# Four attention and aggregation layers on one core: loads, held instructions and idle-time products at three layer passages

## The chip, the cores and the metric

The kernel runs on one core of a Trainium2 chip. The metric is the device time of one execution in microseconds (us). Before the change the median of three runs is 3238.4 us (3236.99 to 3240.71). One more execution, the one that the hardware profiler recorded, took 3230.94 us; all durations quoted from the profile belong to it.

The engines are named as in the profile: PE (TensorE, the matrix engine), DVE (VectorE), ACT (ScalarE), POOL (GpSimd) and SP (SyncE). Each works through its own list of instructions in a fixed order. POOL and SP issue most of the DMA transfers here.

## The reference

A graph of 3327 nodes with 512 features each passes four layers. After each layer the result is added to the layer's input and every row is normalised (mean and variance over the 512 features, no scale or shift). With `x` [3327, 512] and `adj` [3327, 3327] of zeros and ones:

```python
# layers 0, 2 (8 heads of 64) and 3 (4 heads of 128): graph attention
Wh = h @ W                                   # per head
e = leaky_relu(f1[:, :, None] + f2[:, None, :], 0.2)   # f1 = Wh.a1, f2 = Wh.a2
att = softmax(where(adj > 0, e, -9e15), axis=-1)
out = att @ Wh                               # layers 2 and 3: elu(out)
# layer 1: mean over the first 64 neighbours of each row, two linear maps
keep = Ab & (cumsum(Ab, axis=1) <= 64)
xj = leaky_relu((keep @ X) / max(cnt, 1) @ W_nb.T + b_nb)
out = leaky_relu(X @ W_line.T + b_line) + where(cnt > 0, xj, 0)
# after every layer
x = layernorm(x + out)
```

## The kernel before

**Tiles.** Rows are padded to 26 tiles of 128 (`NT` = 26, `HALF` = 13, `IW` = 1664 = 13 tiles). A tile of node features is 128 x 512 in float32.

**An attention layer** (L0, L2 and L3) has a projection stage and an attention stage. In the projection stage each tile is transposed on PE through the identity matrix (`project1`, L267, buffer `pt`), copied to SBUF by ACT (L268, `xT`) and multiplied by the weights `wsb` (`project2`, L277, 16 products into the banks `pw0` and `pw1`). ACT then takes the last columns as exponents and copies (`dc` L278, `rc` and `qc` L281), and DVE scales the projected rows (`vt`, L283). In the attention stage of L0 and L2 (`unit8`, L791 and on) eight units run one after another; each has 26 steps j over the source tiles. Per step DVE makes the weighted mask `t` (L833), ACT the second factor `y` (L834), PE multiplies `t` into four accumulators `po` (L855, 16 products) and `y` into the denominators `pd` (L811). Units 1 to 6 take one head for all 26 target tiles; the first and the last unit, 0 and 7, take two heads (k = 0 and 1) for one half of the targets, so that a step has two DVE and two ACT instructions of half width. At the end of a unit the accumulators are copied (`ob`, L870), transposed by PE (L875), copied (`hb`, L882) and stored to the DRAM tensor `hd` by SP (L886). After the last unit the denominators are transposed on DVE (L948, L951), reduced (L955), written to DRAM (`dd`, L957) and read back (`pes`, L967).

**The norm between layers** is in `finish_steps` (L164 and on): load a tile `h` from `hd` and the residual `xr`, multiply `h` by the reciprocal denominators (`divide`, L182), for layer 2 an exponential on ACT (`e`, L189), add the residual (L197 and L198 for layer 2, L200 for layer 0), and then `norm_rows` for two tiles at once: statistics on DVE (L152, L153), square root on ACT (L154), reciprocal (L155) and the product with the mean (L158) on DVE, and the normalisation of each tile on ACT (L161, one instruction a tile). The buffers of the two last factors are called `rs`.

**The passages.** A passage is the stretch in which one stage's end and the next stage's start overlap.
- L0 to layer 1 (950 to 990 us): the function `sage`, first part. Per tile PE transposes (L1185), and multiplies by the neighbour weights `wn` (`pz`, L1193) and the line weights `wl` (`pi`, L1196), four products each; ACT copies `pz` (L1197), DVE makes the rest `zs` (L1198) and the line result `xi` (L1200 to L1202). Weights, residual rows and the carries `cy` (L1123) are loaded through POOL's queue, tiles 4 and on of `h` and the neighbour mask `mb` (L1140) through SP's.
- Layer 1 to L2 (1600 to 1635 us): `sage`, second part. Row blocks are summed on PE (`acc`, L1295); as each tile is finished (`output`), two jobs transpose and project it for L2. After the last tile come `mean` (`pm`, L299; in the profile under the bank's name `pw`) and unit 0 of L2.
- L2 to L3 (2388 to 2445 us): the function `third`. PE alternates between the transpose of a tile (L267) and the projection of an earlier one (L277). Tiles are loaded up to three pairs ahead (`load_group`), tiles 2 and 3 through POOL's queue, the others through SP's; the residuals and `wsb` come through POOL's. In the step of tile 14, `L3.prepare` clamps and exponentiates the row factors `rc` of the first 13 tiles (L315, L318) and transposes them through the identity in groups (`quad`, L324 to L327).

**What sets the order.** The program records instructions; a list scheduler then sets each engine's order from its own estimates, and may move an instruction ahead of others that were recorded earlier. `tc.keep_in_program_order(ins)` holds an instruction: held instructions of one engine keep the order in which they were recorded among themselves. Before the change the divisions (L182) of a call with `pinned` set are held when `t0 > 2`: those are tiles 4 to 7 of layer 0's norm, which `sage` calls with `t0 < 6`. In `third` only the first exponential of tile 2 is held.

Of the kernel before, what the change touches and what calls it, by code (L numbers as in the profile page):

```python
# [7 lines left out]
F32 = mybir.dt.float32  # L8
# [5 lines left out]
ALU = mybir.AluOpType  # L14
# [4 lines left out]
P = 128  # L19
# [13 lines left out]
def kernel(  # L33
# [111 lines left out]

    def norm_rows(pool, ys, t0):
        n = len(ys)
        st = pool.tile([P, 4, 6], F32, name="st")
        mv = pool.tile([P, 4, 2], F32, name="mv")
        rs = pool.tile([P, 4, 2], F32, name="rs")  # L150
        for s, y in enumerate(ys):
            nc.vector.bn_stats(out=st[:, s, :], in_=y)  # L152
            nc.vector.bn_aggr(out=mv[:, s, :], in_=st[:, s, :])  # L153
        nc.scalar.activation(rs[:, :n, 0], mv[:, :n, 1], AF.Sqrt, bias=eps)  # L154
        nc.vector.reciprocal(rs[:, :n, 0], rs[:, :n, 0])  # L155
        if t0 + n == NT:
            nc.vector.tensor_tensor(rs[:, n - 1, 0:1], rs[:, n - 1, 0:1], valid, op=ALU.mult)
        nc.vector.scalar_tensor_tensor(rs[:, :n, 1], mv[:, :n, 0], -1.0, rs[:, :n, 0],  # L158
                                       op0=ALU.mult, op1=ALU.mult)
        for s, y in enumerate(ys):  # L160
            nc.scalar.activation(y, y, AF.Identity, bias=rs[:, s, 1:2], scale=rs[:, s, 0:1])  # L161
# [3 lines left out]
    def finish_steps(pool, xin, layer, t0, n, hbufs=6, eng=nc.sync, xbufs=None, xpool=None, ebufs=None, pinned=False,  # L165
# [14 lines left out]
        def divide(s):  # L180
# [3 lines left out]
                                          op=ALU.mult)  # L184
            if pinned and t0 > 2:
                tc.keep_in_program_order(ins)
# [18 lines left out]
        else:  # L205
            for s in range(n):
                steps += [lambda s=s: divide(s), lambda s=s: add(s)]
        steps.append(lambda: norm_rows(pool, ys, t0))
        return ys, steps
# [581 lines left out]
    def unit8(self, pools, n, ring, background, aside, ending=None):  # L791
# [47 lines left out]
        for j in range(NT):  # L839
# [4 lines left out]
            if j not in made:  # L844
                js = (j, j + 1) if not u.wide and j in (0, NT - 2) else (j,)
                for j_ in js:
                    made[j_] = tp.tile([P, 2, IW], F32, name="t"), yp.tile([P, 2, IW], F8, name="y")
                for k in range(1 if u.wide else 2):
                    for j_ in js:
                        weights(j_, *made[j_], k)  # L850
# [254 lines left out]
    def sage(first, first_pool, xin, prev, nxt, wsrc, dst, ring):  # L1105
# [5 lines left out]
        with tc.tile_pool(name="sg_z", bufs=1, reuse_waits="tile") as zp, \  # L1111
# [14 lines left out]

            load_carry()
            load_carry()
            zs_ = [zp.tile([P, HALF, 2, F], F32R, name=f"zs{i}") for i in range(2)]
# [40 lines left out]

            for t in range(0, NT, 2):
                load_block(0, t)
            with tc.tile_pool(name="sa_w", bufs=1, reuse_waits="tile") as wp, \
# [5 lines left out]
                blb = wp.tile([P, F], F32, name="blb")  # L1179
                nc.gpsimd.dma_start(out=blb, in_=bl.to_broadcast([P, F]))  # L1180

                def step1(xt):
# [28 lines left out]
                for t0 in range(0, NT, 2):  # L1211
                    ys = ahead
                    if t0 in (6, 10):
                        prev.late.pop(0)(fp)
                    if t0 == 8:
                        cf = fp.tile([NT, P], F32, name="cf", bufs=1)
# [33 lines left out]
            with tc.tile_pool(name="sb_w", bufs=1, reuse_waits="tile") as wp, \  # L1250
# [38 lines left out]
                for b in range(len(blocks)):  # L1289
                    t0, i0 = blocks[b]  # L1290
                    for s in range(G):
# [18 lines left out]

                        def job1(y=y, t=t0 + s, held=held):
                            held["xT"] = nxt.project1(sp, ps, y, t, t < NT - 2)

# [17 lines left out]
    def third(first):  # L1331
        with tc.tile_pool(name="col3", bufs=1) as cp:
# [5 lines left out]
            with tc.tile_pool(name="p_w", bufs=1, reuse_waits="tile") as wp, \  # L1338
# [21 lines left out]
                nc.vector.tensor_copy(wsb[:, :, :, FW:], wa[3].rearrange("p c (e h) -> p c e h", e=2))  # L1360
                load_group(4)
                for t0 in range(0, NT, 2):
                    ys = ahead
# [3 lines left out]
                    for s, y in enumerate(ys):  # L1367
# [10 lines left out]
                        if t == HALF + 1:  # L1378
                            L3.prepare(pp, 0)
                            L3.first_rows = L3.rows(rp, 0, 0)  # L1380
                            L3.cut(pp, 0, "pc", 1, False, True)
# [339 lines left out]
```

## Time and profile before

| | |
|---|---|
| median of three runs | 3238.4 us (3236.99 to 3240.71) |
| the profiled execution | 3230.94 us |
| its span in the profile | 3229.1 us |
| mean granted PE clock | 0.987 of full speed |
| busy share of PE / DVE / ACT / POOL | 97 / 81 / 71 / 8 % |
| waits of PE in 950 to 990 us | 5.5 for `wn`, 1.2 for `h` of L161, 0.5 for `hb`, 0.3 for `xT` |
| waits of PE in 1600 to 1740 us | 3.6 for `rc`, 3.0 for `t`, 1.2 for `pd`, 0.7 for `xT`, 0.7 for `vt` |
| waits of PE in 2395 to 2432 us | 11.2 for `h` of L161, 1.3 for `xr`, 0.2 for `hb` |

The profiled execution lies 7.5 us below the median of the timed runs; times are therefore compared like with like, and a difference worked out in the profile is added to the median. In a timeline row the columns are the start, the duration from the first start to the last end, the engine, the line and operation, the tile written and the tiles read with their shapes, the number of instructions in the row (xN), and in square brackets the idle time of the engine just before it with what ended it. In a list of waits the three numbers after the colon are the sum of the idle time, the number of times and the longest one. An engine's clock in a stretch is given as a share of full speed.

### The profile page before, as it was taken

To read this page: it belongs to the slowest core of one execution; us is meant where nothing else is said; L and a number is where in the kernel's file an instruction comes from. 1 tells how busy PE (TensorE), PEld (TensorE's weight loads), DVE (VectorE), ACT (ScalarE), POOL (GpSimd) and SP (SyncE) were. 2 spreads that over 40 slices of the span, in tenths; PEclk is the share of its full clock that TensorE was granted. 3 is DMA by queue.
4 is the path that set the end of the run, shared out by engine and by line. 5 is a ranking of instruction groups with operands and counts; after the bars stand their busy time and mean duration, and the time that the engine had idled before them with its cause. 6 is when DMAs were issued, how large, how long until landed. Compare 5 with 4: busy or idle time off the path is not lost. (4 is left out here: it accounts for less than half of the span.)

```text
span 3229.1 us, 44980 instructions
## 1 busy us (share of the span) xinstructions
PE 3137.4 (97%) x17910; PEld 1602.3 (50%) x17910; DVE 2626.5 (81%) x2316; ACT 2295.1 (71%) x1855; POOL 266.6 (8%) x414
## 2 busy tenths in 40 slices
PE   8899999999999999999999999999989999999997
PEld 7643343333334467777744333333347655555444
DVE  5799999999987655555499999999999666677887
ACT  1388888899883234444398988899988655568896
POOL 3110000000000111111220000000011000010110
PEclk9999999999999999999999999999999999999998
DMA  9742113111024345555441111011137211122212
GB/s 360 272 149 80 41 51 137 59 45 42 25 87 138 104 127 133 134 142 152 120 135 42 41 35 39 20 42 42 32 107 242 85 43 43 43 59 89 85 47 69
DMA packets 358321, 301.80 MB, mean 93 GB/s; under 512 B 232756, under 2 KB 291966, under 8 KB 356575
## 3 DMA queue, kind: packets, MB, share of 16 engines
q1 hardware_dynamic: 325727, 187.73, 19.9%
q0 software_dynamic: 26864, 103.50, 10.0%
q10 hardware_dynamic: 5520, 7.69, 0.7%
q8 instruction: 142, 2.33, 0.3%
q14 instruction: 68, 0.56, 0.1%
HBM read 221.97 MB, written 76.84 MB: 93 GB/s over the span
## 5 line engine op out<-in xcount | busy, mean ns | idle before, releaser
L834 ACT ACTIVATE y<-t,bi,sc 128x3328 fp8e4<-128x3328 f32 (+1 forms) x520 | 1336.9, 2604 | 100.0 <-PE pd L811 47.8
L855 PE MATMUL po<-t,vj 128*64 128x448 f32 (+1 forms) x6656 | 1272.9, 522 | 14.6 <-DVE t L833 14.5
L855 PEld LDWEIGHTS po<-t,vj 128*64 128x64 f32 x6656 | 461.0, 137 | 687.8 <-issue 617.6
L470 PE MATMUL po<-t,vj 128*128 128x448 f32 (+1 forms) x1456 | 523.3, 516 | 6.2 <-DVE ob L500 3.6
L408 DVE SCALAR_TENSOR_TENSOR t<-rba,qc,mk 128x1664 f32<-128x1664 f32 (+2 forms) x234 | 408.2, 1753 | 127.7 <-PE po L470 88.2
L413 ACT ACTIVATE y<-t,bi,sc 128x1664 fp8e4<-128x1664 f32 (+2 forms) x234 | 374.3, 1617 | 182.5 <-DVE t L408 170.8
L470 PEld LDWEIGHTS po<-t,vj 128*128 128x128 f32 x1456 | 272.1, 190 | 241.5 <-issue 149.8
L833 DVE SCALAR_TENSOR_TENSOR t<-rba,qc,mask 128x3328 f32<-128x3328 f32 (+1 forms) x130 | 381.1, 2987 | 5.7 <-PE po L855 4.9
L833 DVE SCALAR_TENSOR_TENSOR t<-rbb,qc,mask 128x3328 f32<-128x3328 f32 (+1 forms) x130 | 379.9, 2982 | 6.8 <-PE po L855 3.2
L833 DVE SCALAR_TENSOR_TENSOR t<-rbb,qc,mk 128x3328 f32<-128x3328 f32 (+1 forms) x130 | 379.2, 2981 | 6.7 <-PE po L855 4.5
L833 DVE SCALAR_TENSOR_TENSOR t<-rba,qc,mk 128x3328 f32<-128x3328 f32 (+1 forms) x130 | 379.7, 2986 | 5.7 <-PE po L855 3.4
L1295 PE MATMUL acc<-zs,kt 128*128 128x512 f32 x1352 | 360.2, 420 | 0.0
L277 PE MATMUL pw<-wsb,xT 128*128 128x264 f32 (+1 forms) x1248 | 301.7, 397 | 8.8 <-DVE vt L283 7.3
L1295 PEld LDWEIGHTS acc<-zs,kt 128*128 128x128 f32 x1352 | 256.0, 190 | 51.8 <-PE pk L1146 0.8
L811 PE MATMUL pd<-y,sden 128*32 128x384 fp8e4 (+1 forms) x3328 | 270.2, 343 | 0.0
L277 PEld LDWEIGHTS pw<-wsb,xT 128*128 128x128 f32 x1248 | 242.1, 197 | 50.9 <-issue 6.5
L1153 ACT CAST pk<-cy 128x512 f32<-128x512 bf16 x169 | 99.1, 587 | 222.6 <-DVE kt L1167 216.1
L1167 DVE SCALAR_TENSOR_TENSOR kt<-pk,mb 128x512 fp32r<-128x512 f32 x169 | 115.5, 684 | 115.4 <-PE pk L1164 114.2
L811 PEld LDWEIGHTS <-sden 128*32 128x32 bf16 x3328 | 89.1, 95 | 165.3 <-issue 149.9
L283 DVE TENSOR_TENSOR vt<-pw,dc 128x256 f32<-128x256 f32 x156 | 58.7, 417 | 70.5 <-ACT dc L278 64.7
L1193 PE MATMUL pz<-wn,xT 128*128 128x512 f32 x208 | 96.0, 605 | 5.9 <-DMA wn<-in_wnT_dram 5.5
L1123 POOL DMA_DIRECT2D cy<-ctd x91 | 68.0, 747 | 371.1 <-ACT pk L1153 304.7
(249 smaller groups left out, 2234.2 us busy)
## 6 DMA issues: line engine op xcount, KB each, us to landing
raw<-in_adjT_dram SPq DMA_DIRECT2D x67, 416.0 KB
vj<-v SPq DMA_DIRECT2D x169, 128.0 KB
cy<-ctd POOLq DMA_DIRECT2D x78, 256.0 KB, 4.3
h<-hd SPq DMA_DIRECT2D x61, 256.0 KB
v<-vt SPq DMA_DIRECT2D x50, 256.0 KB
xr<-x POOLq DMA_DIRECT2D x45, 256.0 KB, 3.2
md<-mask SPq DMA_DIRECT2D x26, 416.0 KB
mb<-md SPq DMA_DIRECT2D x169, 64.0 KB
```

The lines of the kernel that those rows point to most:

```text
L277: nc.tensor.matmul(pw[e][:, :FW + H], xT[:, c, :], wsb[:, c, e, :], start=c == 0, stop=c == FC - 1)
L408: ins = nc.vector.scalar_tensor_tensor(t[:, :w], rb[:, lo:lo + w], self.qc[:, j, h:h + 1], mask_at[0](j, i0 + lo, w), op0=ALU.max, op1=ALU ...
L413: nc.scalar.activation(y[:, :w], t[:, :w], AF.Sigmoid, bias=self.bi[:, j, h:h + 1], scale=self.sc[:, j, h:h + 1], saturate=False)
L470: nc.tensor.matmul(po[c][k * D:(k + 1) * D, :z - a_], vj[:, j % 2, k * D:(k + 1) * D], ts[k][:, a_:z], start=j == 0, stop=j == NT - 1)
L811: nc.tensor.matmul(pd[c][32 * kk:32 * kk + 32, :w_], lhsT, rhs, start=(kk, c) not in seen, stop=last and j == NT - 1)
L833: nc.vector.scalar_tensor_tensor(to, ro, self.qc[:, j, h:h + 1], m, op0=ALU.max, op1=ALU.mult)
L834: nc.scalar.activation(yo, to, AF.Sigmoid, bias=self.bi[:, j, h:h + 1], scale=self.sc[:, j, h:h + 1], saturate=False)
L855: nc.tensor.matmul(po[c][k * D:(k + 1) * D, :z - a_], vj[:, j % 2, x_:x_ + D], t[:, k, a_:z], start=j == 0, stop=j == NT - 1)
L1153: nc.scalar.copy(pks[k % 2], carry[b, t // 4 * 4][:, t % 4:t % 4 + 2, :])
L1167: nc.vector.scalar_tensor_tensor(kt, pk, NEIGHBOURS, mb[:, t:t + 2, :], op0=ALU.is_le, op1=ALU.mult)
L1193: nc.tensor.matmul(pz, xT[:, c, :], wn[:, c, :], start=c == 0, stop=c == FC - 1)
L1295: nc.tensor.matmul(acc, kts[b, t][:, s * P:(s + 1) * P], zs(t, c), start=t == 0 and c == 0, stop=t == NT - 1 and c == 1)
```

## The change

It has five parts.

1. `unit8`: for the steps in which two tiles are made together (j = 0 and j = 24 of units 0 and 7) the order of recording changes from "k = 0 of both tiles, then k = 1 of both" to "both k of the first tile, then both of the second".
2. `sage`: the loads of `wn`, `wl` and `blb` are recorded ahead of the first two loads of `cy` and of the 13 loads of `mb`. The two `cy` loads are now recorded at t0 = 2 and 4 of the tile loop.
3. `norm_rows` can hold its reciprocal and the product behind it (L155 and L158 before). It does so for layer 2 and t0 = 0, 2 and 4. The divisions that are held are now those of layer 2 with t0 = 2 and 4; layer 0's no longer are.
4. `third`: in the step of tile 14 only the clamp and exponential of `rc` are recorded; the transposes in groups, the other factors and what follows them (`rows`, `cut`) are recorded in the step of tile 15.
5. A helper `warm` multiplies the identity by itself. It is called for 11 products of 128 columns ahead of the transposes of tile 25 in the second part of `sage`, into a buffer of its own with the shape of `acc`, and for 11 more in `third` after `load_group(4)`, into the bank `pw0`.

```diff
--- before.py
+++ after.py
@@ -143,8 +143,13 @@
             eng.dma_start(out=t[:, :, e, :FW], in_=src[:, e * FW:(e + 1) * FW].rearrange("(c p) m -> p c m", p=P))
 
 
-    def norm_rows(pool, ys, t0):
+    def warm(a, n):
+        for _ in range(n):
+            nc.tensor.matmul(a[:, :P], ident, ident, start=True, stop=True)
+
+    def norm_rows(pool, ys, t0, pinned=False):
         n = len(ys)
+        keep = tc.keep_in_program_order if pinned else lambda ins: ins
         st = pool.tile([P, 4, 6], F32, name="st")
         mv = pool.tile([P, 4, 2], F32, name="mv")
         rs = pool.tile([P, 4, 2], F32, name="rs")
@@ -152,11 +157,11 @@
             nc.vector.bn_stats(out=st[:, s, :], in_=y)
             nc.vector.bn_aggr(out=mv[:, s, :], in_=st[:, s, :])
         nc.scalar.activation(rs[:, :n, 0], mv[:, :n, 1], AF.Sqrt, bias=eps)
-        nc.vector.reciprocal(rs[:, :n, 0], rs[:, :n, 0])
+        keep(nc.vector.reciprocal(rs[:, :n, 0], rs[:, :n, 0]))
         if t0 + n == NT:
             nc.vector.tensor_tensor(rs[:, n - 1, 0:1], rs[:, n - 1, 0:1], valid, op=ALU.mult)
-        nc.vector.scalar_tensor_tensor(rs[:, :n, 1], mv[:, :n, 0], -1.0, rs[:, :n, 0],
-                                       op0=ALU.mult, op1=ALU.mult)
+        keep(nc.vector.scalar_tensor_tensor(rs[:, :n, 1], mv[:, :n, 0], -1.0, rs[:, :n, 0],
+                                            op0=ALU.mult, op1=ALU.mult))
         for s, y in enumerate(ys):
             nc.scalar.activation(y, y, AF.Identity, bias=rs[:, s, 1:2], scale=rs[:, s, 0:1])
 
@@ -182,7 +187,7 @@
             ins = nc.vector.tensor_tensor(h.rearrange("p (h d) -> p h d", h=H), h.rearrange("p (h d) -> p h d", h=H),
                                           rec[:, t0 + s, :H].rearrange("p (h e) -> p h e", e=1).to_broadcast([P, H, D]),
                                           op=ALU.mult)
-            if pinned and t0 > 2:
+            if layer.li == 2 and t0 in (2, 4):
                 tc.keep_in_program_order(ins)
             if layer.elu:
                 e = pool.tile([P, F], F32, name="e", bufs=ebufs)
@@ -205,7 +210,7 @@
         else:
             for s in range(n):
                 steps += [lambda s=s: divide(s), lambda s=s: add(s)]
-        steps.append(lambda: norm_rows(pool, ys, t0))
+        steps.append(lambda: norm_rows(pool, ys, t0, layer.li == 2 and t0 < 6))
         return ys, steps
 
     def finish(*a):
@@ -845,8 +850,8 @@
                 js = (j, j + 1) if not u.wide and j in (0, NT - 2) else (j,)
                 for j_ in js:
                     made[j_] = tp.tile([P, 2, IW], F32, name="t"), yp.tile([P, 2, IW], F8, name="y")
-                for k in range(1 if u.wide else 2):
-                    for j_ in js:
+                for j_ in js:
+                    for k in range(1 if u.wide else 2):
                         weights(j_, *made[j_], k)
             t, y = made.pop(j)
             for c, (a_, z) in enumerate(CUTS):
@@ -1124,8 +1129,6 @@
                                     .rearrange("(o t) i -> o t i", o=1).to_broadcast([P, n, GW]))
                 carry[b, t] = cy
 
-            load_carry()
-            load_carry()
             zs_ = [zp.tile([P, HALF, 2, F], F32R, name=f"zs{i}") for i in range(2)]
 
             def zs(t, c):
@@ -1168,8 +1171,6 @@
                                                op0=ALU.is_le, op1=ALU.mult)
                 kts[b, t], kts[b, t + 1] = kt[:, 0, :], kt[:, 1, :]
 
-            for t in range(0, NT, 2):
-                load_block(0, t)
             with tc.tile_pool(name="sa_w", bufs=1, reuse_waits="tile") as wp, \
                     tc.tile_pool(name="sa", bufs=2, reuse_waits="tile") as fp, \
                     tc.tile_pool(name="sa_t", bufs=2, reuse_waits="tile") as sp, \
@@ -1178,6 +1179,8 @@
                 wl = load_w(wp, wlT, "wl", nc.gpsimd)
                 blb = wp.tile([P, F], F32, name="blb")
                 nc.gpsimd.dma_start(out=blb, in_=bl.to_broadcast([P, F]))
+                for t in range(0, NT, 2):
+                    load_block(0, t)
 
                 def step1(xt):
                     pt = ps.tile([P, FC, P], F32, name="pt")
@@ -1212,6 +1215,8 @@
                     ys = ahead
                     if t0 in (6, 10):
                         prev.late.pop(0)(fp)
+                    if t0 in (2, 4):
+                        load_carry()
                     if t0 == 8:
                         cf = fp.tile([NT, P], F32, name="cf", bufs=1)
                         nc.scalar.copy(cf, cr)
@@ -1309,6 +1314,8 @@
                         held = {}
 
                         def job1(y=y, t=t0 + s, held=held):
+                            if t == NT - 1:
+                                warm(ps.tile([P, F], F32, name="acc", bufs=2), 11)
                             held["xT"] = nxt.project1(sp, ps, y, t, t < NT - 2)
 
                         def job2(t=t0 + s, held=held):
@@ -1359,6 +1366,7 @@
                 load_wide(wsb, w3, nc.gpsimd)
                 nc.vector.tensor_copy(wsb[:, :, :, FW:], wa[3].rearrange("p c (e h) -> p c e h", e=2))
                 load_group(4)
+                warm(bank(0), 11)
                 for t0 in range(0, NT, 2):
                     ys = ahead
                     if t0 in (4, 8):
@@ -1376,7 +1384,11 @@
                             L3.project2(pp, bank, wsb, *pend)
                         pend = (xT, t)
                         if t == HALF + 1:
-                            L3.prepare(pp, 0)
+                            steps3 = L3.prepare_steps(pp, 0)
+                            steps3.pop(0)()
+                        if t == HALF + 2:
+                            for f in steps3:
+                                f()
                             L3.first_rows = L3.rows(rp, 0, 0)
                             L3.cut(pp, 0, "pc", 1, False, True)
                     if t0 == 0:
```

Lines after the change are numbered higher by 5 in most of the code (L182 becomes L187, L155 becomes L160, L833 becomes L838, L948 becomes L953), and by 3 in the tile loop of `sage` (L1193 becomes L1196).

## The prediction

> **What bounds the kernel now.** I read the page first, then the lists of waits and the timelines of the passages.
>
> ```profile
> PE 3137.4 (97%) x17910; PEld 1602.3 (50%) x17910; DVE 2626.5 (81%) x2316; ACT 2295.1 (71%) x1855; POOL 266.6 (8%) x414
> ```
>
> PE is busy 97% of the span: inside the long stages a faster other engine is worth little. All that this change can move lies where PE idles, and that is at the passages. Waits of PE, 950 to 990 us, then 2395 to 2432 us:
>
> ```profile
> PE pz L1193 <- DMA wn<-in_wnT_dram: 5.5, 1, 5.5
> PE pt L1185 <- ACT h L161: 1.2, 2, 0.8
> ```
>
> ```profile
> PE pt L267 <- ACT h L161: 11.2, 3, 8.3
> PE pt L875 <- DMA xr<-x: 1.3, 1, 1.3
> ```
>
> The first passage waits for weights, the third for normalised tiles. PE's timeline there shows three waits and what follows a long one: eight transposes take 1.97 us instead of 1.36.
>
> ```profile
> 2410.03 1.97 PE L267 MATMUL pt<-ident,h 128*128 128x128 f32 x8 [8.29 <-ACT h L161]
> 2411.82 8.50 PE L277 MATMUL pw<-wsb,xT 128*128 128x260 f32 x32
> 2422.86 1.36 PE L267 MATMUL pt<-ident,h 128*128 128x128 f32 x8 [2.55 <-ACT h L161]
> 2424.20 5.46 PE L277 MATMUL pw<-wsb,xT 128*128 128x260 f32 x16
> 2429.99 0.66 PE L267 MATMUL pt<-ident,h 128*128 128x128 f32 x4 [0.33 <-ACT h L161]
> ```
>
> DVE's timeline of the same stretch says why the first tile is late:
>
> ```profile
> 2403.74 1.90 DVE L182 TENSOR_TENSOR h<-h,rec 128x512 f32<-128x512 f32 x3 [0.95 <-DMA h<-hd]
> 2405.55 0.16 DVE L155 RECIPROCAL rs<-rs 128x2 f32<-128x2 f32 x1
> 2408.36 0.69 DVE L182 TENSOR_TENSOR h<-h,rec 128x512 f32<-128x512 f32 x1 [2.65 <-DMA h<-hd]
> 2408.97 0.15 DVE L158 SCALAR_TENSOR_TENSOR rs<-mv,rs 128x2 f32<-128x2 f32 x1
> ```
>
> The root was there at 2403.65, but the last factor stands behind the division of tile 6, which waits for its load. Further on, a DVE row from 970 to 990 us, and the PE rows of the second passage and of the row factors:
>
> ```profile
> 976.85 0.16 DVE L158 SCALAR_TENSOR_TENSOR rs<-mv,rs 128x2 f32<-128x2 f32 x1
> ```
>
> ```profile
> 1607.71 0.66 PE L267 MATMUL pt<-ident,y 128*128 128x128 f32 x4 [3.60 <-ACT rc L281]
> 1609.10 5.34 PE L277 MATMUL pw<-wsb,xT 128*128 128x264 f32 x16 [0.73 <-ACT xT L268]
> ```
>
> ```profile
> 2479.80 1.87 PE L324 MATMUL pr<-ident,rc 128*4 128x128 f32 x8 [4.31 <-ACT rc L318]
> ```
>
> **What the Trainium skill says.** "TensorE: Matmul & The Clock Gate", Part 1: PE falls to half its clock after about 3.4 us of idleness and needs about 3.4 us of work to leave it. The trace agrees (clock 0.50 from 2406 to 2412 after 8.29 us), but pw at 2424.20 was slow (5.46 against 3.67) after only 2.55 us. "DMA: Bandwidth & Descriptors", Issuing engines are not separate DMA queues: all issuers share the same 16 DMA engines and interleave. Agreed: 2403 to 2412 shows all 16 busy (341 to 389 GB/s), and tile 6's load, issued by SP at 2399.94, was usable at 2408.36, 8.4 us later. "Perfetto Trace Analysis", Tensor Engine Instruction: ACT and DVE are strict FIFOs. Agreed: the 0.15 us factor above sits out a load that it doesn't need. So I compared the changed build's instruction order, engine by engine, with the old one.
>
> **Part 1, j-first recording.** In unit 7 DVE idles 1.01 us before step 3 (for ACT's y of step 0); y of step 0, k = 1 is now second instead of third on ACT, so this goes: 1.0. At the unit's end PE idled 1.2 (945.86, 2390.92) for the third of four DVE instructions and now needs only two: 1.2. L0 and L2 thus each end 2.2 earlier; both are counted inside the passage that follows. In unit 0 of L0 PE starts 1.9 (one DVE instruction) earlier, but waits 3.0 for DVE at 230 to 250 us anyway, where DVE waits for raw adjacency: 0 (bounds 0 and -1.9).
>
> **Part 2, first passage.** POOL issued wn at 954.37, after two cy issues (1.52). Now wn goes first, and the wait it shares with cy ends 2.2 earlier: 950.7. It took 8.3 to land, beside cy; so it lands by 959 at the latest, and the idle stays short enough that pz(0) runs at 3.7, not 5.81. Taken alone this saves 5.5 + 2.1. But the divisions of layer 0's tiles 4 to 7 aren't held any more, and the new order puts them ahead. On DVE the factors of tiles 2 and 3 (at 976.85) now follow the divisions of tiles 4, 5 and 6; on ACT the norms of tiles 4 to 7 precede the copy xT(2), which pz(2) needs. So pz(2) hangs on tile 6's load, T. SP issued that group at 972.09 to 973.94; it stays behind mask loads that wait, by the program's semaphores, for earlier SP transfers to land, and the crowd of loads starts about 3 us earlier: issued near 969; four 256 KB loads and two cy (1.5 MB at about 370 GB/s) take 4: T = 973 (971 to 975). From T to xT(2): thirteen DVE steps of 0.60 and six of 0.1 (8.4), a root 0.3, one more 0.6 and two factors 0.2, two ACT normalisations 1.5, a copy 0.5: 11.5. pz(2) starts at 984.5, where it was 980.44: +4.1. PE idles some 8 us from pt(3) on, so pz(2) runs at the half clock as pz(0) did: +2.1; the 0.80 that PE waited for tile 4 goes. **Sum +5.4** (+1 to +9). Behind xT(2) on ACT nothing else is late; PE has all it needs from there.
>
> **Part 5, second passage.** Eleven identity products (a 128-column transpose lasts 0.15 to 0.16 in its row of four; ten more behind it: estimate 1.4) go into the 3.60 idle and cut it to 2.2. They wait for nothing. DVE's second instruction of unit 0 waited 1.43 for PE's mean, because its buffer lies over wsb; recorded j-first, the second writes the first tile's buffer and doesn't wait: -1.4. DVE has no other wait for PE in unit 0, and PE idles 1.2 for DVE at that unit's end, so this 1.4 is kept. If the clock is kept too, pw of tile 25 saves 5.34 - 3.72 = 1.6; as a 2.55 idle was followed by a slow pw, I count half. **Sum -2.2** (-3.0 to -1.4).
>
> **Parts 3 and 5, third passage.** Tile 6's division still stands ahead of reciprocal and product of tiles 0 and 1: holding these two against each other buys nothing, the load does. It comes 2.2 earlier (part 1), so pt(0) starts at 2407.8. The warm-up products (1.5, no wait) fall at 2400, before an idle of still some 6 us, and keep no clock: 0. Next, DVE's order puts the divisions of tiles 7 to 11 ahead of the residual step of tiles 2 and 3 (before: up to tile 10). Loads 10 and 11 now follow, on SP, the two x3 stores and dd: issued about 2411, 4 us each: 2415.5. Then two divisions' remainder 0.6, six 0.6 steps, one vt 0.4, root 0.3, three vt 1.1, factors 0.3, ACT 0.8: pt(2) at 2422.6, against 2422.86. The gain of part 1 is eaten (bounds 2420 to 2425).
> Then the held divisions bite. Those of tiles 4 and 5 ran at 2403.74; held, they follow the factors of tiles 2 and 3. And DVE's order now puts the vt of tile 2 ahead of tile 4's last addition: that vt needs the whole of pw(2). PE's own order is pt(2), pt(3), pw(2), pt(4), pw(3). So from pw(2)'s end to pt(4) lie dc 0.35, fourteen DVE steps of 0.60 (8.4), two vt of 0.38, five small ones 0.5, one ACT norm 0.8: 10.8 us of idle PE, where 0.33 stood. pt(2) 2422.6 + 1.4 + pw(2) 4.6 (between 3.67 and 5.46) + 10.8 puts pt(4) at 2439.4 instead of 2429.99: +9.4. At half clock pt(4) and pw(3) lose as pt(0) to pw(1) did (0.6 + 1.2): +1.8. The 0.66 that PE waited for tile 12 (2462.43) is covered by the later PE. **Sum +10.5** (+7 to +14).
>
> **Part 4, row factors.** PE idled 0.76 + 4.31 + 0.40 + 0.43 here, and pr, pt and pw after it ran slow (pw 4.41 against 3.67). Now pt(15) and pw(14), 4.3 us of PE work, stand before the transposes; that covers ACT's exponential. Two copy waits of 0.4 stay; the issue of rr stores and the rows that POOL fetches moves 4 us later, with 30 us left until L3 starts at 2525. **Sum -4.5** (-6 to -3.5).
>
> **Total.** 5.4 - 2.2 + 10.5 - 4.5 = +9.2. Against its own time the profiled execution becomes 3230.9 + 9.2 = 3240.1; the median of the runs, 7.5 above, becomes 3238.4 + 9.2 = 3247.6. Of the bounds, all at the good end give 1 - 3 + 7 - 6 - 1.9 = -2.9, all at the bad end +18; the forecast's own range is 3242 to 3256.
>
> **Rivals.**
> - *Early weights win (not slower).* Tile 6's load lands before PE has finished tile 1. At T = 962 pz(2) follows pt(3) directly and passage one saves 7.6 instead of costing 5.4: 3238.4 + 9.2 - 13.0 = 3234.6. From T near 965 down the total is below zero. For it: two cy loads (0.5 MB), beside which the DMA engines moved only 118 to 121 GB/s from 956.4 to 958.1, are out of the way. Against: SP's transfers crawl beside wn and wl (ACT waited for an hd store of this passage until 971.50), and those two still come.
> - *Both passages gain.* The orders cost nothing because waits in front are shorter than I think: passage one -7.6, passage three -2.2 and its 2.55 idle: 3238.4 - 7.6 - 2.2 - 4.8 - 4.5 = 3219. For it: 5.5 and 11.2 us of PE waits are there to be won. Against: the order of DVE at tile 4, which is certain.
> - *The change doesn't do what it says.* Held factors come no earlier, no clock is kept, and the loads hide tile 4's chain by half: 5.4 - 1.4 + 4 - 4.5 = +3.5: 3242.
>
> **How the numbers follow.** Forecast 0.64, early weights 0.13, both gain 0.10, not as said 0.13. About 0.2% (6.5 us) is what a measurement of this kernel can tell from no change. Of the forecast 0.58 lies over +6.5, 0.06 within; early weights and "not as said" fall within (0.03 of the latter over): slower 0.61, same 0.27, faster 0.12 with "both gain" and a share of early weights. The range 3234 to 3257 holds forecast and both middle rivals and leaves out some 0.2.
>
> **What would show it.** Right: in the new trace wn's wait nearly gone, pz(2) after an idle of 6 to 10 us ended by ACT's xT, pt(4) of layer 3 after some 11 us ended by ACT's h, the 4.31 before pr gone, DVE's 1.43 at unit 0 gone. Wrong: a short idle at pt(4) or at pz(2).

## The result, and the profile after it

The change makes the kernel slower. The changed kernel takes 3252.4 us (median of six runs, 3250.5 to 3258.2) where the kernel before takes 3237.8 (3234.8 to 3244.1): ratio 1.0044, 95% interval 1.0034 to 1.0054, some 14.6 us. The forecast was 3247.6, a change of +9.2, with a range of 3234 to 3257 and 0.61 on "slower".

The profiled execution of the changed kernel took 3254.97, 24.0 more than the profiled one of before. Most of the distance between 24.0 and 14.6 lies in the first profile of before, which was a low run. A second profile of that kernel (last experiment) took 3240.66, and against it the difference is 14.3. The table gives, by stage, how much later PE is than in the first profile of before. A stage is the time between the same instruction of PE in both kernels; its number is the growth of that delay.

| stage, from PE's timelines | before, second profile | after | after, again | forecast |
|---|---|---|---|---|
| start to the first transpose of `ob` after L0 | -1.0 | -2.5 | -2.8 | -2.2 |
| from there to tile 10 of layer 1 (first passage) | +0.6 | +10.1 | +10.0 | +7.6 |
| rest of layer 1, to the transpose of tile 25 | +7.1 | +4.6 | +6.3 | 0 |
| from there to the end of unit 0 of L2 (second passage) | +0.2 | +0.8 | +0.1 | -2.2 |
| to the first transpose of `ob` after L2 | +2.2 | +3.3 | +1.6 | -2.2 |
| from there to tile 10 of layer 3 (third passage) | 0.0 | +14.8 | +17.3 | +12.7 |
| from there to the mean of L3 (row factors) | +0.7 | -7.6 | -7.5 | -4.5 |
| rest | 0.0 | +0.4 | -0.5 | 0 |

In the forecast's own words the first two rows are its "+5.4", and the two around L2's end its "+10.5". The rest of layer 1 moves by 7 between two runs of the kernel before, and L0 and L2 by 1 to 2: such amounts can't be put down to the change. The rows of the passages are steadier between the two profiles of before (0.6 at most), but the two of the changed kernel differ by 2.5 in the third passage, where projections of the second profile ran slow for longer (10.34 for the 8.71 and 6.13 for the 5.00 of the first).

PE in the first passage of the changed kernel:

```profile
957.94 5.26 PE L1196 MATMUL pz<-wn,xT 128*128 128x512 f32 x8 [0.69 <-ACT xT L1190]
...
976.52 1.36 PE L1188 MATMUL pt<-ident,h 128*128 128x128 f32 x8 [1.78 <-ACT h L166]
986.41 6.38 PE L1196 MATMUL pz<-wn,xT 128*128 128x512 f32 x8 [8.53 <-DVE xi L1205]
```

The wait of 5.5 for the weights is gone, and one of 8.53 has come in before `pz` of tile 2. Its releaser is named as DVE's `xi`, but ACT's copy of `xT` for tile 2 ran at 985.80, 0.6 before `pz`; that was the last one needed. DVE's timeline there:

```profile
972.32 0.69 DVE L187 TENSOR_TENSOR h<-h,rec 128x512 f32<-128x512 f32 x1 [6.76 <-DMA h<-hd]
...
974.87 0.67 DVE L187 TENSOR_TENSOR h<-h,rec 128x512 f32<-128x512 f32 x1
975.46 0.15 DVE L163 SCALAR_TENSOR_TENSOR rs<-mv,rs 128x2 f32<-128x2 f32 x1
```

Divisions of tiles 4 and 6 run ahead of the last factor of tiles 2 and 3, as the forecast said, but the load that DVE sat on, for 6.76, is tile 4's; tile 6's division follows at 974.9 without a wait (forecast 973), and 11.5 later PE goes on.

PE in the second passage, and ACT's copy of the mean:

```profile
1616.22 2.62 PE L148 MATMUL acc<-ident 128*128 128x128 f32 x22
1619.98 0.66 PE L272 MATMUL pt<-ident,y 128*128 128x128 f32 x4 [1.15 <-ACT rc L286]
1621.65 3.83 PE L282 MATMUL pw<-wsb,xT 128*128 128x264 f32 x16 [1.01 <-ACT xT L273]
```

```profile
1631.08 0.66 ACT L306 ACTIVATE ms<-pw 128x256 f32<-128x256 f32 x2 [4.57 <-DMA v<-vt]
```

The eleven products hold the clock: `pw` of tile 25 takes 3.83, not 5.34. But ACT then waits 4.57 (2.59 before) for a store of `vt`, whose buffer `ms` takes over, and by the end of unit 0 the gain is gone.

PE and DVE in the third passage:

```profile
2426.16 1.97 PE L272 MATMUL pt<-ident,h 128*128 128x128 f32 x8 [1.58 <-ACT h L166]
2429.34 8.71 PE L282 MATMUL pw<-wsb,xT 128*128 128x260 f32 x32 [1.21 <-ACT xT L273]
2441.22 1.36 PE L272 MATMUL pt<-ident,h 128*128 128x128 f32 x8 [3.17 <-ACT h L166]
2442.55 5.42 PE L282 MATMUL pw<-wsb,xT 128*128 128x260 f32 x16
2459.41 1.11 PE L272 MATMUL pt<-ident,h 128*128 128x128 f32 x4 [11.43 <-ACT h L166]
```

```profile
2424.29 0.69 DVE L187 TENSOR_TENSOR h<-h,rec 128x512 f32<-128x512 f32 x1 [4.66 <-DMA h<-hd]
...
2448.22 0.42 DVE L288 TENSOR_TENSOR vt<-pw,dc 128x256 f32<-128x256 f32 x1 [1.69 <-ACT dc L283]
2448.56 0.68 DVE L203 SCALAR_TENSOR_TENSOR h<-h,xr 128x512 f32<-128x512 f32 x1
```

The held factors of tiles 0 and 1 still follow a division that waits for tile 6's load (first DVE row). `pt` of tile 4 waits 11.43 (forecast 10.8): `vt` of tile 2, which needs the end of `pw` at 2448.0, stands ahead of tile 4's last addition (last two rows). `pt` and `pw` on both sides of that wait run slow. And the row factors, where 4.31 stood before `pr`:

```profile
2509.42 1.04 PE L329 MATMUL pr<-ident,rc 128*4 128x128 f32 x8
```

### The profile page after: what moved, and what is told of

Read it like the earlier page. It is cut to its first block, busy times and chain, and to the rows that moved or that the text cites. A ratio compares the mean times of both kernels' runs of the same rounds, so it can differ in the third digit from the quotient of the medians.

```text
span 3253.3 us, 45064 instructions
## 1 busy us (share of the span) xinstructions
PE 3149.7 (97%) x17954; PEld 1611.4 (50%) x17954; DVE 2626.0 (81%) x2316; ACT 2291.7 (70%) x1853; POOL 269.8 (8%) x414
## 5 line engine op out<-in xcount | busy, mean ns | idle before, releaser
L838 DVE SCALAR_TENSOR_TENSOR t<-rbb,qc,mk 128x3328 f32<-128x3328 f32 (+1 forms) x130 | 379.3, 2983 | 10.3 <-PE po L860 7.3
L838 DVE SCALAR_TENSOR_TENSOR t<-rba,qc,mask 128x3328 f32<-128x3328 f32 (+1 forms) x130 | 380.9, 2984 | 5.7 <-PE po L860 4.9
L838 DVE SCALAR_TENSOR_TENSOR t<-rba,qc,mk 128x3328 f32<-128x3328 f32 (+1 forms) x130 | 379.5, 2983 | 5.9 <-PE po L860 5.0
L838 DVE SCALAR_TENSOR_TENSOR t<-rbb,qc,mask 128x3328 f32<-128x3328 f32 (+1 forms) x130 | 379.8, 2983 | 5.0 <-DMA mask<-nb 1.8
L1196 PE MATMUL pz<-wn,xT 128*128 128x512 f32 x208 | 98.1, 616 | 10.2 <-DVE xi L1205 8.5
```

What stands on the lines that cost most here:

```text
L838: nc.vector.scalar_tensor_tensor(to, ro, self.qc[:, j, h:h + 1], m, op0=ALU.max, op1=ALU.mult)
L1196: nc.tensor.matmul(pz, xT[:, c, :], wn[:, c, :], start=c == 0, stop=c == FC - 1)
```

## The experiments

Theory: the release of layer 0's divisions costs the first passage and the holds cost the third; the other parts gain. Rivals: the new order of the loads, transfers that land late, or the identity products cost it. "Delay" below is a growth as in the table. Ratios are against the kernel before, run on the same chip; in the diffs a minus is the kernel that the text starts from.

**1. Layer 0's divisions held again.**

```diff
-            if layer.li == 2 and t0 in (2, 4):
+            if pinned and t0 > 2 or layer.li == 2 and t0 in (2, 4):
```

> The changed kernel, with layer 0's divisions of tiles 4 to 7 held again as before; all else as changed. My theory (the order of DVE and ACT that came with the release costs the first passage): the 8.5 us idle before pz of tile 2 goes, pz of tile 2 follows pt of tiles 2 and 3 within 1 us and at full clock (3.7), PE later waits some 1 to 1.5 us for tile 4; the passage ends 3 to 4 us earlier than in the kernel before instead of 7.6 later, so about -11 against the changed kernel: 3241 (3239 to 3245). Rival (the new order of the loads, mask and neighbour weights, costs the passage): PE still waits 6 us or more before pz of tile 2 or of tile 4, time within 3 us of the changed kernel's 3252.

Measured: 3242.6, ratio 1.0011 (1.0004 to 1.0017), so about -12 against the changed kernel's 1.0049 in the same runs. The first passage's delay falls from +10.1 to +0.1; the rows around tile 2 have no long idle:

```profile
974.38 1.04 PE L1188 MATMUL pt<-ident,h 128*128 128x128 f32 x8
975.71 3.70 PE L1196 MATMUL pz<-wn,xT 128*128 128x512 f32 x8 [0.29 <-ACT xT L1190]
...
985.71 0.66 PE L1188 MATMUL pt<-ident,h 128*128 128x128 f32 x4 [2.86 <-ACT h L166]
```

The release is the cost. But the early weights leave nothing either: without the release the passage is as long as before. Experiment 11 comes back to that.

**2. No holds in the third passage.**

```diff
-            if layer.li == 2 and t0 in (2, 4):
+            if False:
-        steps.append(lambda: norm_rows(pool, ys, t0, layer.li == 2 and t0 < 6))
+        steps.append(lambda: norm_rows(pool, ys, t0))
```

> The changed kernel without any hold on layer 2's norm (no held factors, no held divisions of tiles 2 to 5); layer 0's release, loads, row factors and identity products as changed. My theory (the holds let tile 4's additions fall behind vt of tile 2): the 11.4 us idle before pt of tile 4 goes, PE's waits in the third passage are again some 8 + 2.5 us before pt(0) and pt(2), and the time falls by 13 (11 to 16): 3239. Rival (the loss there comes from transfers that land later, since SP's stores and loads are crowded): an idle of 6 us or more stays between pt(2) and pt(6), and the time falls by less than 6.

Measured: 3249.8, ratio 1.0034 (1.0022 to 1.0047): only about 5 below the changed kernel. A miss: 13 was expected. The 11.4 before `pt` of tile 4 goes, but the third passage still has a delay of +5.0, with an idle of 3.97 before `pt` of tile 6, and the row factors save 3.3 instead of 7.6. Fallen: that the holds are the whole loss of the third passage.

**3. The changed kernel again.**

> The changed kernel once more, for a second profile of it. What belongs to the change (8.5 us before pz of tile 2, 3.2 before pt of tiles 2 and 3 of layer 3, 11.4 before pt of tile 4, ACT's 4.6 at ms) should stand again within 0.5 us; the 3.4 us that DVE waited at 1511 for a transfer that the change does not touch, and the single slow rows between 1750 and 2320 us, should not, if they are scatter. Time 3252 (1.0044 of the kernel before).

Measured: 3254.8, ratio 1.0049 (1.0036 to 1.0063). Waits: 8.07 before `pz` of tile 2, 3.17 and 11.43 in the third passage, 4.64 at `ms`: as in the first profile. The wait for `yx` near 1511, expected to go, stood again (3.82 on DVE), so this run left open whether it is scatter; experiment 12 settles it.

**4. Part 3 undone** (experiments 1 and 2 together).

> The changed kernel with part 3 wholly undone: layer 0's divisions held as before, nothing held in layer 2. Parts 1, 2, 4 and 5 stay. My theory: the two orders are the whole loss and they add up, so 3252 - 11 - 13 = 3228 (3223 to 3232), faster than the kernel before by 0.2 to 0.4%. Rival (the identity products or the later row factors cost something too, or the freed time turns into a wait for loads): not faster than 3235.

Measured: 3237.1, ratio 0.9995 (0.9984 to 1.0007). No faster than before: the rival's side. Its stages against before: first passage 0.0, second -1.7, third +5.4, row factors -4.1. So with part 3 gone the third passage still loses 5, and what remains of the change eats its own gain.

**5. The holds of layer 2 alone**, on the kernel before.

```diff
-            if pinned and t0 > 2:
+            if pinned and t0 > 2 or layer.li == 2 and t0 in (2, 4):
-        nc.vector.reciprocal(rs[:, :n, 0], rs[:, :n, 0])
+        keep(nc.vector.reciprocal(rs[:, :n, 0], rs[:, :n, 0]))
...
```

> The kernel before with one thing of part 3 alone: the held factors (tiles 0 to 5) and held divisions (tiles 2 to 5) of layer 2's norm. Layer 0's divisions stay held as before. If the holds are what costs the third passage, an idle of 10 to 12 us stands before pt of tile 4 of layer 3, nothing else changes, and the time is 11 to 15 above the kernel before: 3252 (ratio 1.0035 to 1.0046). If the holds cost only the 5 us by which taking them out shortened the changed kernel, it is 3244 (1.0015).

Measured: 3246.8, ratio 1.0038 (1.0026 to 1.0051), the first alternative. The wait stands, smaller than in the changed kernel:

```profile
2445.88 1.11 PE L272 MATMUL pt<-ident,h 128*128 128x128 f32 x4 [8.11 <-ACT h L166]
```

The third passage's delay is +9.9, and the row factors then give 3.3 back, though part 4 is not in this kernel. The profile places 6.7. The medians of the same runs lie 8.1 apart, the ratio stands for 12 (8 to 17) with only five runs of this kernel; how much is left to place is open. The path isn't quite that of the changed kernel either: `vt` of tile 2 runs at 2438.34 without a wait. Held behind the factors of tiles 2 and 3 (2429.16), the division of tile 4 runs only at 2433.09, and from there DVE works on without a gap until tile 4's factors at 2443.91.

**6. The products of the third passage alone**, on the kernel before.

```diff
+                warm(bank(0), 11)
```

> The kernel before with the eleven identity products of the third passage alone (the second half of part 5). In the prediction they cost and gain nothing. The kernel without release and holds still lost 5.4 us in the third passage, and its order of DVE there differs from that of before, with tile 2's vt and tile 3's ahead of work for tiles 4 to 9; the products alone, or the j-first recording alone, give that other order. Theory now: the products cost nothing themselves, but the scheduler answers them with that order, and so an idle of 4 us stands before pt of tile 4, another of 1 to 2 later on, and the time is 5 (3 to 7) above the kernel before: 3244 (1.0010 to 1.0022). Rival (what was lost there came from earlier transfers or from the row factors): no idle over 1 us before pt of tile 4, time within 2 us of before.

Measured: 3247.2, ratio 1.0028 (1.0017 to 1.0039), some 9 (6 to 13) where 5 (3 to 7) was expected. The third passage's delay is +6.5: eleven products whose result nobody reads go with a loss of that size. The idle stands before `pt` of tile 6, not of tile 4, and its cause is not tile 3's `vt`:

```profile
2453.14 1.11 PE L272 MATMUL pt<-ident,h 128*128 128x128 f32 x4 [4.24 <-ACT h L166]
```

```profile
2443.38 0.69 DVE L187 TENSOR_TENSOR h<-h,rec 128x512 f32<-128x512 f32 x1 [4.40 <-DMA h<-hd]
```

The DVE row is the division of tile 12. DVE's orders of the built kernels (d: division of a tile, a: last addition, n: last factor of two tiles; `vt`s and what isn't needed left out):

```
before, and 7, 8, 10, 11:  a2 a3 a4 n2 a5 d11 a6 n4 a7 d12 a8 n6
products or j-first alone: d11 a2 a3 a4 n2 a5 n4 d12 a6 a7 a8 n6
```

In the second order tile 12's division comes ahead of all that tile 6 still needs, and its load isn't there: it uses the buffer of tile 2 (ten `h` buffers) and can start only once tile 2 has been transposed and stored. Before, that division ran at 2430.74 without a wait, after the last additions of tiles 6 and 7. No run has the products together with the first order, so the order as the cause is read from the traces. Experiments 2, 4 and 9 have the second order too, with an idle of 3.97, 4.25 and 3.61 before `pt` of tile 6; in the kernels with the first order that idle is absent.

**7. The row factors a tile later, alone**, on the kernel before (part 4 of the diff).

> The kernel before with part 4 alone: the transposes of the row factors and what follows them are recorded one tile later. The prediction said -4.5 (-6 to -3.5); the changed kernel's profile shows 8.6 saved by tile 16 and 1.1 given back by tile 20. In that kernel the saving may include some that only refunds what the late third passage had cost DVE and ACT. If the step is worth what the sum said, the time is 4.5 below the kernel before (0.9986) and the idle of 4.3 before pr is gone; if it is worth what the changed profile shows, 7.5 (0.9977).

Measured: 3235.6, ratio 0.9992 (0.9981 to 1.0003). The interval takes in no change and the sum's 4.5, but not 7.5. The profile shows -5.5 by tile 16; then 0.9 and 1.0 are given back (`pw` waits 0.62 and 0.58 for `xT`): -3.6 by the mean of L3.

**8. What seemed good, combined.** Against the changed kernel:

```diff
-            if layer.li == 2 and t0 in (2, 4):
+            if pinned and t0 > 2:
-        steps.append(lambda: norm_rows(pool, ys, t0, layer.li == 2 and t0 < 6))
+        steps.append(lambda: norm_rows(pool, ys, t0))
-        def mean(self, pool, bank, wsb):
+        def mean(self, pool, bank, wsb, tag="vt"):
...
-            ms = pool.tile([P, F], F32, name="ms", tag="vt")
+            ms = pool.tile([P, F], F32, name="ms", tag=tag)
-                for j_ in js:
-                    for k in range(1 if u.wide else 2):
-                        weights(j_, *made[j_], k)
+                for j_, k in ([(a, k) for a in js for k in range(1 if u.wide else 2)] if self.li == 0 or n == 0 else
+                              [(a, k) for k in range(1 if u.wide else 2) for a in js]):
+                    weights(j_, *made[j_], k)
-                nxt.mean(sp, bank, wsb)
+                nxt.mean(sp, bank, wsb, "xi")
-                warm(bank(0), 11)
```

> What the runs so far say is good, put together: the weights first with layer 0's divisions still held; j-first recording in all units but the last one of layer 2 (there it turns the order of the third passage); the products of the second passage; the row factors a tile later; no holds and no products in the third passage; and the buffer of the mean's row (ms) no longer lies over the projected rows of tile 24 but over an earlier xi, so that ACT needn't wait for their store. Expected by the sums: first passage -3, second -2.2 kept now that ACT's wait of 4.6 at ms is gone (ms within 1 us of pm), third 0, row factors -4.5: 3239 - 9.7 = 3229 (3225 to 3233; 0.9970). Rival for the second passage (DVE or the store of the mean holds unit 0 back anyway): unit 0 ends no earlier against its pm than in the kernel before (117.2 us after it).

Measured: 3230.4, ratio 0.9976 (0.9969 to 0.9984): faster than both. First passage +0.3 (-3 was expected), second -1.7, third +0.4, row factors -3.2. Of the 1.7 in the second passage the kept clock saves 1.5, ahead of the mean. For unit 0 itself the rival was right: it ends 117.1 after the mean's start, as before (117.2), although ACT no longer waits for the store and DVE no longer for the mean. ACT here, then DVE before (first two rows) and here:

```profile
1621.66 0.38 ACT L306 ACTIVATE ms<-pw 128x256 f32<-128x256 f32 x1 [1.34 <-PE pw L304]
```

```profile
1618.92 9.40 DVE L833 SCALAR_TENSOR_TENSOR t<-rba,qc,mk 128x1664 f32<-128x1664 f32 x5 [1.43 <-PE pw L299]
...
1637.83 0.36 DVE L371 TENSOR_TENSOR rest<-rest,pc 128x104 f32<-128x104 f32 x1 [0.63 <-ACT pc L370]
```

```profile
1640.40 0.36 DVE L376 TENSOR_TENSOR rest<-rest,pc 128x104 f32<-128x104 f32 x1 [2.06 <-ACT pc L375]
```

The second half of `ms` starts 3.76 after the mean's start in both kernels, and ACT then goes on without a gap. DVE's 1.43 wait for the mean is gone, but its wait for ACT's `pc` has grown from 0.63 to 2.06, by the same 1.43.

**9. The j-first recording alone**, on the kernel before (part 1 of the diff).

> The kernel before with part 1 alone (j-first recording in units 0 and 7 of L0 and L2). The prediction's terms: L0 and L2 each end 2.2 earlier, unit 0 of L2 saves 1.4, so -4 to -6 if nothing eats it (0.9984). Theory now: L0's 2.2 to 2.8 stay; the 1.4 of unit 0 does not (DVE then waits as much longer for ACT's pc); and this recording, like the eleven products, turns the scheduler's order of DVE in the third passage: the factors of tile 6 come behind tile 3's vt, PE idles some 4 us before pt of tile 6, and from the end of L2 to tile 10 of the third passage the kernel loses 5 to 6. Sum about +2 (-1 to +5): 3241 (1.0006).

Measured: 3242.3, ratio 1.0026 (1.0017 to 1.0034): +8, above the expected +2 (-1 to +5); the medians lie 6.6 apart. The mechanism is there: third passage +5.7, 3.61 before `pt` of tile 6, tile 12's division after a wait of 2.90. L0 ends 2.2 earlier than in the first profile of before (experiments 6 and 10, without this recording, do too), and the first passage is 1.2 longer. The profile places 5.7 of the 8.

**10. The release alone**, on the kernel before.

```diff
-            if pinned and t0 > 2:
+            if False:
```

> The kernel before with layer 0's divisions of tiles 4 to 7 no longer held, and nothing else: the weights and all loads as before. If the release is what costs the first passage, the cost stands here too: the tile-6 load, issued at 972 to 974, lands at about 977, pz of tile 2 starts 11.5 later at 988.5 instead of 980.4 and runs slow (6.4), so +10 (8 to 12): 3249 (1.0031). If it cost only together with the new order of the loads, an idle of under 3 us before pz of tile 2 and a time within 3 us of before.

Measured: 3244.2, ratio 1.0024 (1.0015 to 1.0032). First passage +8.7, with 5.55 before `pz` of tile 2, which then takes 5.78:

```profile
985.80 5.78 PE L1198 MATMUL pz<-wn,xT 128*128 128x512 f32 x8 [5.55 <-ACT xT L1192]
```

The release costs by itself; the loads' order isn't needed.

**11. The combined version, and one copy of ACT held.**

```diff
-                        nc.scalar.copy(cf, cr)
+                        tc.keep_in_program_order(nc.scalar.copy(cf, cr))
```

> The combined version with one more hold: ACT's copy cf<-cr, which stands ahead of the square root for tiles 2 and 3 and waits 4.3 us for the load of cr (in the first experiment until 971.2), is held, and so stands 25 instructions later. Theory: the 5.5 that the early weights save is eaten there: root, factors and zs of DVE, and with them tile 4's normalisation, wait behind cr, so PE's 2.9 before pt of tile 4 is this wait. Then it goes here, the first passage ends 2.5 to 3 earlier than in the combined version, and the time is 3227.5 (ratio 0.9967 against 0.9976). Rival: tile 4 waits for its own load from SP's queue; then the 2.9 stays and the time is that of the combined version.

Measured: 3226.3, ratio 0.9966 (0.9954 to 0.9978), as expected, and the lowest ratio of all, though its interval and that of experiment 8 (0.9969 to 0.9984) overlap; what separates the two is the profile. ACT in experiment 1, then in this one:

```profile
971.24 0.30 ACT L1222 CAST cf<-cr 26x128 f32<-26x128 bf16 x1 [4.33 <-DMA cr<-ctd]
971.44 0.29 ACT L159 ACTIVATE rs<-mv,eps 128x2 f32<-128x2 f32 x1
```

```profile
967.74 0.30 ACT L159 ACTIVATE rs<-mv,eps 128x2 f32<-128x2 f32 x1
```

The root for tiles 2 and 3 comes 3.7 earlier, PE's 2.86 before `pt` of tile 4 is gone (`983.18 0.66`, no idle), and the first passage is 3.1 shorter than before. This copy, needed only at tile 8, was what took the gain of the early weights. The hold without the early weights wasn't run; in the kernel before PE waited only 0.80 before `pt` of tile 4.

**12. The kernel before again.**

> The kernel before once more, for a second profile of it. Its first profiled execution took 3230.94, 5 to 8 below the medians of its timed runs, so every difference read against that profile is too large by as much. In the second one the waits of the three passages should stand within 0.5 us of the first (5.5 for the weights; 3.6 and 3.0 in the second passage; 8.3, 2.6 and 0.3 in the third; 4.3 before pr), and what is above 3231 should lie elsewhere: in DVE's wait for yx near 1500 (0.2 in the first, 0.8 to 4.6 in the other kernels) and in single slow rows of PE in the long stages.

Measured: 3238.0, ratio 0.9994 (0.9984 to 1.0004). Its waits in the passages: 5.64 for the weights, 3.60 and 3.01, then 7.33, 3.27 and 1.20, 4.31 before `pr`; three of them are off by 0.7 to 1.0, more than I expected, but the third passage is as long as in the first profile. The rest lies where it was expected:

```profile
1503.68 0.71 DVE L263 STREAM_TRANSPOSE xT<-yx 128x512 f32<-128x512 f32 x1 [4.37 <-DMA yx<-x]
```

This wait was 0.17 in the first profile, and 0.75, 4.37 and 0.89 in experiments 5 to 7, whose code is the same up to there.

## Why the prediction was right, point by point

- **First passage, +5.4: right in mechanism, measured +7.6 and +7.2.** Two terms were short. Tile 6's division ran at 974.9, not 973 (the chain of 11.5 behind it was exact), and `pz` lost 2.7 to the clock, not 2.1. The load waited for was tile 4's, not tile 6's. The sentence "Taken alone this saves 5.5 + 2.1" is wrong, though the sum didn't use it: with the release undone the passage saves nothing (experiment 1), because ACT's copy of `cr` comes next (experiment 11). Nor did `pz` of tile 0 run at 3.7: it took 5.26 and 6.62 in the two profiles, after short idles.
- **L0 and L2, -2.2 each: partly.** The 1.2 of PE at both units' ends is gone from the timelines. More can't be told of L0: its end moves by as much in kernels without this part (-2.2 in experiments 6 and 10), and little of it outlives the first passage (-1.0 in experiment 9). L2's 2.2 doesn't show at all (+3.3 and +1.6, where the second profile of before has +2.2).
- **Second passage, -2.2: the step that failed.** The clock was kept, 1.5 instead of the half of 1.6 that I counted. What failed is the 1.4. "DVE has no other wait for PE in unit 0 ... so this 1.4 is kept" looked for waits for PE only; the next wait of DVE is for ACT, and it took all of the 1.43 (experiment 8). In the changed kernel ACT lost more at `ms`, whose buffer waits for a store: the forecast left out whether that store would move with PE. In the changed kernel `ms` starts 4.88 after the mean's start and the stage measures +0.8 (second profile +0.1); in experiments 1 and 4, with the same code here, it starts 3.75 and 3.14 after it, and the stage measures -1.4 and -1.7. So how much of the clock's gain is left hangs on when that store lands.
- **Products of the third passage, 0: wrong as a cost of the part.** They hold no clock there, as I said: `pt` of tiles 0 and 1 takes 1.97 behind them in the changed kernel and in experiment 6 (in experiment 1 it takes 1.36, but the `pw` after it 9.96, where 8.50 stood before). Their cost is in the order that the scheduler gives DVE (experiment 6: +6.5). The sum read DVE's order from the changed build and so may contain the effect, but it put all of it down to the held divisions.
- **Third passage, +10.5: right in mechanism, 2 short.** Counted from the end of L2 the forecast is 10.5 + 2.2 = 12.7; measured 14.8 (17.3 in the second profile). Up to `pt` of tile 2 it looks exact, +1.9 forecast and +1.95 measured, but the second profile has +4.0 there: in part luck. Then `pw` took 5.42 instead of 4.6 and the wait 11.43 instead of 10.8; and the 0.66 that the forecast takes off for tile 12 lies past the end of this row, where a wait of 0.64 (before `pw`, at 2494.00) stands instead. The cause was only in part the one I named. The holds alone make 9.9 (experiment 5, 8.11 at tile 4), without the wait for `vt` of tile 2; taking them out of the changed kernel leaves 5.0 (experiment 2), since the j-first recording or the products then turn the order.
- **Row factors, -4.5: measured -7.6 in the changed kernel, -3.6 alone.** The step is worth 5.5 by tile 16 and gives 1.9 back by the mean of L3, which the forecast hadn't costed. Of the other 4.0, 3.3 is a refund of the holds' loss, as experiment 5 shows without part 4. How the holds bring it about isn't shown.
- **Total: near in part by luck.** The change measured +14.6, the forecast was +9.2. Against the second profile of before the rows of the changed kernel add up to 14.1. In the table's order they erred by +0.7, +1.9, -2.5, +2.8, +3.3, +2.1, -3.8 and +0.4. The -2.5 is the rest of layer 1, which the change doesn't touch, and the -3.8 of the row factors has its cause mostly in the holds' loss; both cancel errors that lie elsewhere.

What stays open: what the timed runs show of the holds alone and of the j-first recording alone beyond the stages (some 1 us by the medians, 3 to 6 by the ratios); why the scheduler turns DVE's order; and an order for the third passage that frees tiles 0 and 1 from tile 6's load, which wasn't tried.

## What to carry to other kernels

When a list scheduler sets an engine's order, cost a change by the order of the whole built kernel: here eleven products whose result nobody reads, or a swap of two loops in another stage, came with an order that puts a division waiting for its load ahead of a tile that PE needs, and lost 5.7 to 6.5 us. When a wait is taken away, read the next wait of every engine on the way (here DVE's for ACT, ACT's for a small load needed only six tiles later), for it decides how much of the gain stays. The early load of the weights gained nothing until one such instruction was moved back; then the passage was 3.1 shorter.

## What the runs showed of the hardware

- A float32 product stands twice in the trace as a matmul: 11 products of the identity with itself are x22, the four of `pz` are x8. The 11 took 2.62 at a granted clock of 1.00 (0.24 each, where I had estimated 1.4 for all) and 4.90 in a stretch with a granted clock of 0.50.
- Put into the idle of 3.60 before tile 25's transposes they left 1.15 of it in the changed kernel. `pw` of tile 25 took 3.83 in each of the seven profiles with these products, and 5.34 to 6.88 in the seven without.
- The clock is lost after shorter idles than I had counted on, and not each time alike. In the changed kernel `pz` of tile 0 took 5.26 though the two idles before it were 2.52 and 0.69; in experiment 1, 6.59 after 2.52 and 1.29. The Trainium skill ("TensorE: Matmul & The Clock Gate", Part 1) says that the activity window is free-running and the number of slow products varies from run to run. The runs agree: after the same wait of 2.52, `pt` of tiles 0 and 1 of layer 1 took 1.97 in one profile of the changed kernel and 1.36 in the other.
- The same transfer can be in time or 4 us late in two runs of one kernel: DVE waited 0.17 and 4.37 for `yx` in the two profiles of before.
